# Exponentials bank by bank and sums in two halves in a windowed-attention softmax

## The chip, the core and the metric

The kernel runs on one core of one Trainium2 chip. The metric is the device time of one execution in microseconds (us); the time before is the median of three runs. One further execution was recorded by the hardware profiler, and all profile lines come from it. Engines are named as the profile names them: PE is TensorE's matrix multiplication and PEld its weight load, DVE is VectorE, ACT is ScalarE, POOL is GpSimd and SP is SyncE.

## The reference

The program is a chain of four residual blocks on an input of 4 x 1024 x 128: a selective state-space scan ("mamba"), a layer of eight experts with two chosen for each token, a dynamic convolution over 31 positions, and a transformer of six layers. Only the transformer's attention is touched:

```python
def local_attention(q, k, v):
    ...
    sim = jnp.einsum('bhwie,bhwje->bhwij', bq, bk2) * QK_SCALE
    sim = jnp.where(mask, -jnp.finfo(sim.dtype).max, sim)
    attn = jax.nn.softmax(sim, -1)
    out = jnp.einsum('bhwij,bhwje->bhwie', attn, bv2)
    return out.reshape(b, h, n, d)
```

There are 16 heads of 64 channels and windows of 32 positions; each position looks at its own window and the one before it, 64 keys in all. So for a tile of 128 positions the softmax is over 128 x 16 rows of 64 values. The kernel computes it as usual: the maximum of a row, the differences to it, their exponentials, the sum of these, and the product with the sum's reciprocal.

## The kernel before

**Tiling.** The transformer works on 192 tiles: 4 sequences by 6 layers by 8 tiles of 128 positions. The loop in `run` (line 1501) takes one tile i per turn. In a turn it turns queries and keys of tile i by transposes (`turn`), makes the scores and the softmax of tile i (`scores`, line 1328), mixes the values of tile i - 1 with its softmax (`mix`, line 1387), and projects tile i + 2 to queries and keys (`project`, line 1256). After every fourth tile a feed-forward block of 512 positions follows, spread over the turns (`feedforward`). Beside the tiles, `along` lets three lines of other work advance a share at a time: mamba, experts and convolution of the later sequences, and the preparation of later layers' weights. That work is used up before the end, so the last tiles run with nothing beside them.

**The softmax of a tile.** `scores` holds the scores in two PSUM banks (`sv`, tile name `sim` in the code, `bank` in the profile): bank e has the even or the odd heads, 8 heads x 64 keys = 512 values in each of 128 partitions. For each bank VectorE takes the maximum into `mx` and subtracts it into `at` (lines 1355 to 1362). `at` is one SBUF buffer of 128 x 1024 values, ordered head pair, bank, key; the half of one bank is 8 pieces of 64 values with a stride of 128. Two such buffers are used in turn. Then follow, over all 1024 values: one exponential on ScalarE (line 1364), one sum over each row of 64 on VectorE into `sm` (line 1366), the reciprocal of the 16 sums (line 1367), and one product on POOL (line 1368). `mix` transposes `at` on PE, ScalarE copies it to `aT`, PE multiplies it with the values into two banks at a time, ScalarE copies these to `zT`, and PE multiplies `zT` with the joined value and output weights `wvo`.

**What else is on these engines.** `project` makes, for each of four half-sized matrix products of a tile: one square on ScalarE (`sq`), two products with the rotary tables on VectorE (`r`, `rb`), one sum of the squares on VectorE (into `words`). Then POOL adds `r` and `rb`, VectorE finds 32 inverse roots in small steps (`root`, `ne`, `words`), and POOL multiplies `r` with them. `feedforward` has three Gelu functions for each 512 positions (`ge`), and the experts have them too (`ehg`). ScalarE holds one table of functions at a time; a change between the table with Exp and that with Gelu is an instruction of its own (ACT_TABLE_LOAD in the profile). The copies and squares are not tied to a table in the planner's accounts.

**Who sets the order.** No call in these functions goes to an engine directly. The class `Order` takes each operation as a unit with its engine, its cost (`length`, line 248), the units that it depends on (by exact sets of elements, so that two strided halves of one buffer do not touch) and its PSUM banks. `arrange` (line 278) then plans the whole program at once: at each step it gives out the unit that can start earliest, among those that start nearly as early the one first written, with limits on free banks and on how far ahead it may look (500 units). A unit that needs another function table than the one loaded counts 1.28 us later (line 319). `give` (line 369) issues the units in the planned order, each engine's queue in order; the waits between engines are drawn from the dependencies. As every instruction is issued on line 374, the profile's groups all bear that line and are told apart by tile names. The planner counts a reduction on VectorE of n values, up to 1024, at 0.07 + 0.00104 n us, and a function on ScalarE at 0.25 + 0.00045 n us up to 512 values and 0.25 + 0.0007 n above.

Of the kernel before, what the change touches and what calls it, by code (L numbers as in the profile page):

```python
# [10 lines left out]
F32 = mybir.dt.float32  # L11
BF16 = mybir.dt.bfloat16
I32 = mybir.dt.int32
AF = mybir.ActivationFunctionType
ALU = mybir.AluOpType
AX = mybir.AxisListType
PSUM = bass.MemoryType.PSUM

P = 128
# [11 lines left out]
DEPTH, HEADS, DH, WIN = 6, 16, 64, 32  # L31
# [1118 lines left out]
class Transformer:  # L1150
# [177 lines left out]
    def scores(self, t, qT, kT):  # L1328

        nc, c = self.nc, self.c
        m = self.mask[:, 0 if t == 0 else 1, None, :].to_broadcast([P, 8, 2 * WIN])
        sv = [c.bank("sim").rearrange("p (a k) -> p a k", k=2 * WIN) for e in range(2)]
        with nc.together(2.0):
            for e in range(2):
                nc.tensor.matmul(
                    sv[e], self.identb, m, start=True, stop=False, skip_group_check=True
                )
            for a in range(8):  # L1340
                for g in range(4):
                    for e in range(2):
                        rows = slice(e * 64, (e + 1) * 64)
                        cols = slice(g * WIN, (g + 1) * WIN)
                        nc.tensor.matmul(
                            sv[e][cols, a, :],
                            qT[rows, a, cols],
                            kT[rows, a, g * WIN : (g + 2) * WIN],
                            start=False,
                            stop=True,  # L1350
                            skip_group_check=True,
                        )
        mx = self.sb.tile([P, 2, 8], F32, "mx", bufs=3)
        at = self.sb.tile([P, 8, 2, 2 * WIN], F32, "at", bufs=2)
        for e in range(2):
            nc.vector.tensor_reduce(out=mx[:, e, :], in_=sv[e], op=ALU.max, axis=AX.X)
            nc.vector.tensor_tensor(
                out=at[:, :, e, :],
                in0=sv[e],
                in1=mx[:, e, :, None].to_broadcast([P, 8, 2 * WIN]),  # L1360
                op=ALU.subtract,
            )
        av = at.rearrange("p a e k -> p (a e) k")
        nc.scalar.activation(av, av, AF.Exp)
        sm = self.sb.tile([P, HEADS], F32, "sm", bufs=3)
        nc.vector.tensor_reduce(out=sm, in_=av, op=ALU.add, axis=AX.X)
        nc.vector.reciprocal(sm, sm)
        nc.gpsimd.tensor_tensor(
            out=av, in0=av, in1=sm[:, :, None].to_broadcast([P, HEADS, 2 * WIN]), op=ALU.mult
        )  # L1370
        return at
# [359 lines left out]
```

## Time and profile before

| what | value |
|---|---|
| time, median of three runs | 4260.55 us (4259.56 to 4266.35) |
| the profiled execution's time | 4259.06 us |
| its span in the trace | 4257.2 us |
| instructions in it | 112033 |
| mean granted clock of PE | 0.948 |

How to read what follows. A line with percentages gives each engine's busy time in us, its share of the span and the number of its instructions. The rows of forty digits cut the span into equal slices of 106 us, each digit being the busy share in tenths. A row of a group gives the engine, the operation, output and input by name, their shapes and the count; then, behind the bar, the total busy time in us and the mean of one instruction in ns; then, behind the next bar, the time that the engine stood idle just before such instructions and what ended most of it. A row of the waits gives who waited, for whom, the total in us, the number of times and the longest. Duration and pace differ: on VectorE and ScalarE the next instruction can begin before the last one's recorded end.

### The profile page before, as it was taken

The page shows a single profiled execution, that of the slowest core. Times are in us where ns is not written, and L with a number is a line of the kernel's source. Part 1 is how long each engine was busy: PE and PEld are TensorE (multiplying, and loading weights), DVE is VectorE, ACT ScalarE, POOL GpSimd, SP SyncE. Part 2 cuts the span into 40 slices and gives each one's busy share as a digit, 9 for nine tenths or more (in the row PEclk, how much of TensorE's full clock was granted, in tenths as well). Part 3 has the DMA queues.
Part 4 walks back from the last instruction along what each step waited for, and adds up shares of the span by engine and source line. Part 5 has one row for each costly group of instructions (what it writes and reads, how often), then busy time and mean ns, then how long its engine had stood idle before and what let it go on. Part 6 is the DMA issues. An engine that isn't in the chain of part 4 may idle for free. (4 is left out here: it accounts for less than half of the span.)

```text
span 4257.2 us, 112033 instructions
## 1 busy us (share of the span) xinstructions
PE 3801.6 (89%) x45306; PEld 2721.5 (64%) x45317; DVE 3612.4 (85%) x9374; ACT 2610.7 (61%) x4854; POOL 2964.5 (70%) x1832
## 2 busy tenths in 40 slices
PE   3874788998988999988999999999999999999997
PEld 1762465675665666656676677766666777777775
DVE  4668789888997879999998787898989898888985
ACT  3754466675555777655667676666665666666664
POOL 3388667666878766777789665788688666666663
PEclk6886899999998999989999999999999999999998
DMA  3323321222112221111113122121111010101100
GB/s 91 104 83 123 119 85 43 86 62 72 60 68 82 91 73 55 45 57 53 44 63 114 58 65 63 41 73 59 58 61 51 27 41 25 32 21 34 33 27 11
DMA packets 136878, 261.25 MB, mean 61 GB/s; under 512 B 16112, under 2 KB 93992, under 8 KB 129192
## 3 DMA queue, kind: packets, MB, share of 16 engines
q1 hardware_dynamic: 123352, 211.47, 15.0%
q0 software_dynamic: 13008, 42.62, 3.2%
q8 instruction: 357, 5.85, 0.6%
q14 instruction: 161, 1.32, 0.1%
HBM read 224.41 MB, written 29.62 MB: 60 GB/s over the span
## 5 line engine op out<-in xcount | busy, mean ns | idle before, releaser
L374 POOL TENSOR_TENSOR r<-r,rb 128x1024 f32<-128x1024 f32 x384 | 906.9, 2367 | 365.2 <-DVE rb L374 297.9
L374 POOL TENSOR_TENSOR r<-r,root 128x1024 f32<-128x1024 f32 x384 | 723.2, 1903 | 181.2 <-DVE root L374 154.4
L374 PE MATMUL bank<-wqk,hs 128*128 128x512 f32 x1536 | 769.7, 624 | 45.0 <-DVE at L374 13.3
L374 PEld LDWEIGHTS bank<-zT,wvo 128*128 128x128 f32 x6144 | 723.2, 194 | 88.8 <-issue 53.2
L374 PE MATMUL bank<-zT,wvo 128*128 128x128 f32 x6144 | 729.4, 277 | 6.5 <-ACT zT L374 3.5
L374 ACT ACTIVATE sq<-bank 128x512 f32<-128x512 f32 x768 | 450.4, 601 | 458.1 <-DVE words L374 228.1
L374 ACT COPY zT<-bank 128x512 f32<-128x512 f32 x768 | 403.7, 597 | 382.4 <-PE bank L374 376.6
L374 DVE TENSOR_TENSOR r<-bank,rot 128x512 f32<-128x512 f32 x768 | 522.0, 680 | 103.4 <-issue 36.2
L374 POOL TENSOR_TENSOR at<-at,sm 128x1024 f32<-128x1024 f32 x192 | 365.4, 1903 | 326.2 <-DVE sm L374 146.3
L374 DVE TENSOR_TENSOR rb<-bank,rot 128x512 f32<-128x512 f32 x768 | 520.8, 678 | 62.8 <-ACT sq L374 53.8
L374 DVE TENSOR_REDUCE words<-sq 128x8 f32<-128x512 f32 x768 | 526.5, 686 | 14.3 <-ACT sq L374 5.3
L374 PEld LDWEIGHTS bank<-wqk,hs 128*128 128x128 f32 x1536 | 267.6, 195 | 322.7 <-issue 157.7
L374 PE MATMUL bank<-aT,xw 64*128 64x256 f32 x3072 | 430.6, 404 | 25.4 <-DVE at L374 10.3
L374 PE MATMUL bank<-ident,r 128*128 128x128 f32 x3080 | 400.6, 278 | 45.1 <-DVE rb L374 10.0
L374 PEld LDWEIGHTS bank<-ident,r 128*128 128x128 f32 x3080 | 350.1, 143 | 134.9 <-issue 59.7
L374 PEld LDWEIGHTS bank<-aT,xw 64*128 64x128 f32 x3072 | 295.6, 192 | 153.2 <-issue 44.3
L374 PEld LDWEIGHTS bank<-kT,qT 64*32 64x32 f32 x24576 | 259.7, 106 | 106.8 <-issue 105.4
L374 PE MATMUL bank<-kT,qT 64*32 64x64 f32 x24576 | 296.6, 227 | 12.4 <-issue 11.9
L374 DVE TENSOR_REDUCE mx<-bank 128x8 f32<-128x512 f32 x384 | 254.1, 680 | 44.4 <-PE bank L374 44.3
L374 PE MATMUL bank<-fxn,w 128*128 128x512 f32 (+1 forms) x576 | 272.8, 607 | 7.0 <-ACT fxn L374 4.8
L374 ACT ACTIVATE at<-at 128x1024 f32<-128x1024 f32 x192 | 203.5, 1060 | 117.6 <-DVE at L374 83.2
L374 ACT COPY qT<-bank 128x512 f32<-128x512 f32 x384 | 228.3, 600 | 66.2 <-PE bank L374 62.8
(207 smaller groups left out, 6849.8 us busy)
## 6 DMA issues: line engine op xcount, KB each, us to landing
near<-rows SPq DMA_DIRECT2D x31, 1024.0 KB
near<-rows SPq DMA_DIRECT2D x31, 960.0 KB
rot<-rotd SPq DMA_DIRECT2D x192, 128.0 KB
wqk<-in_Wqkv SPq DMA_DIRECT2D x48, 512.0 KB
wvo<-wvod SPq DMA_DIRECT2D x24, 1024.0 KB
ewt<-in_w_ex SPq DMA_DIRECT2D x16, 514.0 KB
w<-in_W SPq DMA_DIRECT2D x24, 341.0 KB
wvod<-eT SPq DMA_DIRECT2D x24, 256.0 KB
```

The costliest lines, as they stand in the source:

```text
L374: getattr(engine, op)(*map(real, args), **{k: real(v) for k, v in kw.items()})
```

## The change

The exponential over both banks becomes one for each bank, written directly behind that bank's subtraction. The sum over all 16 heads becomes two sums over 8 heads, one for each bank, written after both; each writes every second value of `sm`. The reciprocal and the product stay as they are. The values computed are the same.

```diff
         mx = self.sb.tile([P, 2, 8], F32, "mx", bufs=3)
         at = self.sb.tile([P, 8, 2, 2 * WIN], F32, "at", bufs=2)
+        sm = self.sb.tile([P, HEADS], F32, "sm", bufs=3)
+        sums = sm.rearrange("p (a e) -> p a e", e=2)
         for e in range(2):
             nc.vector.tensor_reduce(out=mx[:, e, :], in_=sv[e], op=ALU.max, axis=AX.X)
             nc.vector.tensor_tensor(
@@ -1360,10 +1362,10 @@
                 in1=mx[:, e, :, None].to_broadcast([P, 8, 2 * WIN]),
                 op=ALU.subtract,
             )
+            nc.scalar.activation(at[:, :, e, :], at[:, :, e, :], AF.Exp)
+        for e in range(2):
+            nc.vector.tensor_reduce(out=sums[:, :, e], in_=at[:, :, e, :], op=ALU.add, axis=AX.X)
         av = at.rearrange("p a e k -> p (a e) k")
-        nc.scalar.activation(av, av, AF.Exp)
-        sm = self.sb.tile([P, HEADS], F32, "sm", bufs=3)
-        nc.vector.tensor_reduce(out=sm, in_=av, op=ALU.add, axis=AX.X)
         nc.vector.reciprocal(sm, sm)
         nc.gpsimd.tensor_tensor(
             out=av, in0=av, in1=sm[:, :, None].to_broadcast([P, HEADS, 2 * WIN]), op=ALU.mult
```

## The prediction

> **What bounds the kernel now.** I read the busy table of the page first, then its slices, then the table of stretches, and only then the groups. Busy time and slices say that no engine is the bound throughout:
>
> ```profile
> PE 3801.6 (89%) x45306; PEld 2721.5 (64%) x45317; DVE 3612.4 (85%) x9374; ACT 2610.7 (61%) x4854; POOL 2964.5 (70%) x1832
> ...
> PE   3874788998988999988999999999999999999997
> PEld 1762465675665666656676677766666777777775
> DVE  4668789888997879999998787898989898888985
> ```
>
> The table of stretches (start:end, then busy us of PE, PEld, DVE, ACT, POOL, then clock, DMA share and GB/s) separates the two parts in which the softmax runs:
>
> ```profile
> 600.00:3400.00 2800.00, 2586.64 (x31617) 1852.36 (x31627) 2456.19 (x6357) 1790.24 (x3366) 2072.56 (x1262) 0.97 0.19 62
> 3400.00:4200.00 800.00, 786.17 (x10510) 577.92 (x10495) 711.82 (x1811) 507.59 (x900) 512.36 (x289) 1.00 0.09 29
> ```
>
> In the last 800 us PE is busy for 98.3% (786.17 of 800): nothing to be had but 13.8 us. In the 2800 us before it, where mamba, experts and conv run beside the tiles, PE is idle for 213.4 us and VectorE for 343.8 us. What PE waited for, over the whole span (engine waiting, releaser, us, times, longest):
>
> ```profile
> PE bank L374 <- DVE m L374: 63.7, 52, 11.4
> PE bank L374 <- DVE at L374: 38.7, 40, 5.2
> ...
> PE bank L374 <- ACT zT L374: 13.1, 25, 1.2
> ...
> PE bank L374 <- POOL at L374: 8.6, 12, 2.5
> ```
>
> The second row is a wait for the subtraction, which frees the score bank; the change does not touch when a subtraction may begin. The last two are what it can shorten: POOL's product is the end of the softmax, and the exp stands ahead of copies to zT in ScalarE's queue. Together 21.7 us.
>
> **The change, part by part.** The rows are these, counts and mean ns ahead of and behind the bar's busy time:
>
> ```profile
> L374 ACT ACTIVATE at<-at 128x1024 f32<-128x1024 f32 x192 | 203.5, 1060 | 117.6 <-DVE at L374 83.2 <-DVE ne L374 19.8 <-DVE words L374 5.6
> L374 DVE TENSOR_REDUCE sm<-at 128x16 f32<-128x1024 f32 x192 | 232.5, 1211 | 28.8 <-ACT at L374 27.1
> ...
> L374 ACT ACTIVATE ew<-ew 128x496 f32<-128x496 f32 x32 | 19.8, 620 | 42.3 <-DVE ew L374 36.0 <-DVE ne L374 6.1
> ```
>
> *The sums.* 192 reductions of 128x1024 go, 384 of 128x512 come. The nearest row is the reduction of sq in `project`, also from SBUF, 768 times at 686 ns. By durations: 2 x 686 - 1211 = +161 ns, 30.9 us in all. But durations overlap on VectorE, as the timeline shows:
>
> ```profile
> 3878.49 1.21 DVE L374 TENSOR_REDUCE sm<-at 128x16 f32<-128x1024 f32 x1
> 3879.61 0.68 DVE L374 TENSOR_REDUCE words<-sq 128x8 f32<-128x512 f32 x1
> 3880.20 0.24 DVE L374 RECIPROCAL sm<-sm 128x16 f32<-128x16 f32 x1
> ```
>
> The instruction after a full sum starts 1.12 us later, that after a half-sized one 0.59 us later; the medians of all such pairs that I read are 1.13 and 0.60. So a tile costs 2 x 0.60 - 1.13 = +0.07 us of VectorE, 13.4 us over 192 tiles. Here a rule speaks against the change: the Trainium skill, Perfetto Trace Analysis, section "Optimizing Scalar/DVE Operations", gives each VectorE instruction about 60 ns of data access on SBUF and each ScalarE one about 93 ns, and advises grouping work into larger operations where an engine is saturated. By it the sums cost 192 x 60 ns = 11.5 us, by the row 13.4; I take the row. The rule's condition is what matters: VectorE is at 88% (2456.19 of 2800) in the mixed part and 89% in the last. In the mixed part some 135 of the 192 tiles run (the products by window), so all of it on the path would be 135 x 0.07 = 9.5 us; in the last part PE covers it. I take half, **+5 us** (ends 0, if all is hidden, and +22, which is 135 x 161 ns).
>
> *The exps.* 192 of 128x1024 go, 384 of 128x512 come. By the row of ew (128x496) 2 x 620 - 1060 = +180 ns, in pace 2 x 0.53 - 0.96 = +0.10 us, so 19 us of ScalarE (the same rule would say 17.9). ScalarE is busy 64% in the mixed part and 63% in the last, so PE's and VectorE's work hide this; were that cover gone it would be 19 us, 35 by the durations.
>
> *The gain.* A softmax is shorter from the second subtraction to the product: about 0.43 us of exp (0.96 - 0.53), as the first half runs beside the second maximum and subtraction, and, where VectorE is free, the first sum beside the second exp (another 0.5 us). The chain of waits shows where the exp alone holds PE:
>
> ```profile
> 3689.86 1.21 DVE at L374 x2
> ...
> 3691.14 1.06 ACT at L374
> 3692.20 0.48 ACT zT L374
> ```
>
> The copy to zT waits behind the exp, the exp for both subtractions; with halves zT starts some 0.4 us sooner, if the planner leaves it there. In 62 of 192 tiles the instruction after the exp on ScalarE is such a copy. A third of the 13.1 us behind zT is 4.2 us; of the 8.6 us behind the product I count 2, since before many products the sum stands in VectorE's queue behind r, rb and words long after its exp is done. **-6 us** (ends 0 and -21.7).
>
> *The waits.* ScalarE's second exp waits for the second subtraction while sq (93 tiles) or zT (62) is queued behind it, as behind the one exp now; the new one is the first exp's wait for its own subtraction. What follows the first exp may now be held for up to the 1.3 us of maximum and subtraction, if the plan puts both exps side by side. VectorE's first sum waits for the first exp, its second for the second; behind them stand r, rb and words, on which the squares' buffers and POOL's r wait. The 28.8 us of idle time before the sum is what that costs now, and halves can lengthen or shorten it; I take zero net. The reciprocal follows the second sum at once, as it followed the full one. POOL and DMA issue nothing new; the loop over banks moves no transfer past SP or POOL.
>
> *Table loads.* There are 195, 1283 ns each. A Gelu planned between the two exps costs up to two more. In 20 tiles a Gelu stands between the first subtraction's end and the exp. The planner charges 1.28 us to whatever changes the table, so it will rarely split a pair: 0 to 20 x 2 x 1.283 = 51 us of ScalarE; five splits, 13 us, mostly in its idle third: **+2 us**. The skill's ScalarE: Activation LUTs, section "Table sets: the hidden batching unit", says to keep calls of one set together and puts a switch at about 2.7 us; the trace's row is 1.28, so the five splits would be 27 us by the page and 13 by the row.
>
> *The order.* All instructions of all engines come from one plan, and 384 units more of other lengths in it move everything behind them. No row shows that. Bounds: in the last 800 us a better order can win at most 13.8 us; a worse one, with PE as idle as in 3200 to 3400 us (188.69 of 200, 5.7%), loses 32 us; in the mixed part a tenth more or less of PE's 213 us is 21 us either way. The asymmetry of the PE-bound part decides: a third of the 32, **+10 us**.
>
> Sum: 5 - 6 + 2 + 10 = +11 us on the profiled execution's 4259.06 us (span 4257.2), so **4270 us**; the median of the runs, 4260.55, lies 1.5 us above that execution, and I leave this inside the rounding. About 0.2% (8.5 us) is what a measurement of this kernel can tell from no change.
>
> **The rivals.** *Hidden* (23%): the longer sums lie in VectorE's idle time, the order comes out as good, 4260 us. For it: 85% and 61% busy; against: any new order is a throw of more than 8 us. *Shorter chain* (22%): the 21.7 us behind zT and the product go almost whole and the mixed part gains a few us more, about -25, 4235 us. For it: POOL idles 146 us for the sum; against: POOL is not the bound, and the sum is late by VectorE's queue. *Broken rhythm* (13%), on the other side of that: ScalarE stands on its first exp's or second exp's wait with zT behind it, so PE waits for its bank. Price 0.25 us in each of 192 tiles, 48 us, 4308 us; it decides from some 0.1 us a tile, where it alone passes the term for the order. The same price follows if the strided halves of one buffer were ordered against each other, the second subtraction waiting for the first exp: 0.62 + 0.1 of signal - 0.60 of maximum = 0.12 us a tile, 23 us on VectorE. In that case the change does not do what it says. Forecast (small loss): 42%.
>
> So slower by over 0.2% is 0.42 + 0.13 = 0.55, within 0.23, faster 0.22. Range: from near the shorter chain to the broken rhythm, 4238 to 4312; the forecast's own is 4269 to 4290.
>
> **What would show it.** Right: sums at 384 x some 0.68 us, VectorE's busy time up by about 31 us and ScalarE's by about 35, PE at less than 98% in the last 800 us, up to ten more table loads. Wrong: PE's waits for zT and for the product gone with the span below 4250; or table loads up by 20 or more; or second subtractions that VectorE begins only after the first exp ended.

## The result, and the profile after

The changed kernel takes 4281.74 us (median of 5 runs, 4279.02 to 4286.13) against 4259.56 us (4252.49 to 4266.35): ratio 1.0054, 95% interval 1.0041 to 1.0067. It is slower, and about 23 us is to be explained (17 to 29 by the interval). Its profiled execution took 4279.02 us, with a span of 4277.2, 20.0 us above that of before. The busy table:

```profile
PE 3825.2 (89%) x45317; PEld 2726.2 (64%) x45317; DVE 3635.5 (85%) x9566; ACT 2624.8 (61%) x5046; POOL 2970.2 (69%) x1832
```

VectorE is busy 23.1 us longer and ScalarE 14.1 us; both shares of the span are what they were. The table of stretches:

```profile
600.00:3400.00 2800.00, 2588.72 (x31462) 1848.59 (x31461) 2457.82 (x6462) 1792.62 (x3486) 2070.36 (x1258) 0.97 0.19 63
3400.00:4200.00 800.00, 788.56 (x10444) 574.26 (x10429) 719.82 (x1846) 503.71 (x937) 507.95 (x286) 1.00 0.09 29
```

Read the counts, not the busy times. In the last 800 us PE looks busier than before (788.56 for 786.17 us), but it did 10444 matrix products for 10510, and POOL 286 operations for 289: a little less work in the same time. The comparison is rough, as the changed kernel is some 18 us behind by then and the 800 us hold a slightly different piece of it. The softmax's groups and the waits of PE that the prediction named:

```profile
L374 DVE TENSOR_REDUCE sm<-at 128x8 f32<-128x512 f32 x384 | 251.1, 677 | 9.8 <-ACT at L374 8.0
L374 ACT ACT_TABLE_LOAD x195 | 250.2, 1283 | 100.0 <-DVE at L374 96.0 <-PEq L1721 0.7 <-DVE m L374 0.3
L374 ACT ACTIVATE at<-at 128x512 f32<-128x512 f32 x384 | 232.0, 630 | 182.5 <-DVE at L374 123.8 <-DVE ne L374 32.9 <-DVE words L374 23.5
```

```profile
PE bank L374 <- DVE at L374: 43.9, 32, 9.2
...
PE bank L374 <- DVE rb L374: 41.6, 42, 4.9
...
PE bank L374 <- ACT zT L374: 17.4, 32, 1.4
...
PE bank L374 <- POOL at L374: 3.9, 3, 2.7
```

The halves have the lengths that were forecast. Table loads are 195, as before, but ScalarE now stands 100.0 us in front of them, where it stood 4.1. The subtractions end 96.0 us of this, 26 waits of at most 4.1 us: in these tiles the load ahead of a first half-exp starts only once a subtraction is done. Here the first half-exp was planned early, ahead of copies to zT, after a Gelu:

```profile
3871.97 0.69 ACT L374 ACTIVATE ge<-bank,b 85x512 f32<-85x512 f32 x1 [0.17 <-PE bank L374]
3876.62 1.28 ACT L374 ACT_TABLE_LOAD   x1 [3.96 <-DVE at L374]
3877.91 1.15 ACT L374 ACTIVATE at<-at 128x512 f32<-128x512 f32 x2
3878.97 2.03 ACT L374 COPY zT<-bank 128x512 f32<-128x512 f32 x4
```

In another tile both half-exps came between the second and the third copy to zT. The chain of waits there runs through the exps and that copy into PE, which stood 0.19 us for it (start, us, what; in the kernel before, the chain is PE's own work there, 33.12 us from 3827.23):

```profile
3857.32 1.24 ACT at L374 x2
3858.57 0.48 ACT zT L374
3859.05 0.04 issue
3859.09 4.87 PE bank L374 x35
```

That made a tempting story: the first exp, brought forward, blocks ScalarE's queue. What PE stood for it directly is small, though: its waits for zT rose by 4.3 us in all, from 13.1 to 17.4. The experiments had to say whether the story was the loss.

### The profile page after: what moved, and what is told of

The parts are those of the page before. It is cut to its first block, busy times and chain, and to the rows that moved or that the text cites. A ratio compares the mean times of both kernels' runs of the same rounds, so it can differ in the third digit from the quotient of the medians.

```text
span 4277.2 us, 112319 instructions
## 1 busy us (share of the span) xinstructions
PE 3825.2 (89%) x45317; PEld 2726.2 (64%) x45317; DVE 3635.5 (85%) x9566; ACT 2624.8 (61%) x5046; POOL 2970.2 (69%) x1832
## 4 chain that ended last, share of the span: by engine, by line
DVE 37%; PE 30%; ACT 7%; issue 4%; POOL 1%; DMA 1%; ACTq 0%; POOLq 0%; DVEq 0%; SPq 0%
PE bank L374 30%; DVE words L374 8%; DVE rb L374 6%; DVE r L374 6%; DVE sm L374 3%; DVE mx L374 2%; DVE ne L374 2%; DVE hs L374 2%; ACT sq L374 2%; DVE at L374 2%; DVE cxn L374 1%; DVE m L374 1%; DVE st L374 1%; ACT at L374 1%; ACT zT L374 1%
## 5 line engine op out<-in xcount | busy, mean ns | idle before, releaser
L374 PE MATMUL bank<-wqk,hs 128*128 128x512 f32 x1536 | 785.0, 632 | 63.3 <-DVE at L374 26.0
L374 ACT ACTIVATE at<-at 128x512 f32<-128x512 f32 x384 | 232.0, 630 | 182.5 <-DVE at L374 123.8
L374 PE MATMUL bank<-kT,qT 64*32 64x64 f32 x24576 | 297.3, 228 | 11.6 <-issue 11.5
```

The costliest lines, as they stand in the source:

```text
L374: getattr(engine, op)(*map(real, args), **{k: real(v) for k, v in kw.items()})
```

## The experiments

Times drift a little between comparisons, so each run is read as its ratio to the kernel before, run beside it on the same chip.

### The plan and the instructions taken apart

A unit of the planner holds a list of calls. Exchanging the calls after the unit has been recorded keeps the plan and changes what is issued. In the first trace below every instruction of ScalarE, VectorE, POOL and PE's weight loads stands where it stood before, each pair counted as one.

**old_plan_halves**, from the kernel before:

```diff
-        nc.scalar.activation(av, av, AF.Exp)
+        u = nc.scalar.activation(av, av, AF.Exp)
+        u.calls = [("activation", (at[:, :, e, :], at[:, :, e, :], AF.Exp), {}) for e in range(2)]
...
-        nc.vector.tensor_reduce(out=sm, in_=av, op=ALU.add, axis=AX.X)
+        u = nc.vector.tensor_reduce(out=sm, in_=av, op=ALU.add, axis=AX.X)
+        u.calls = [
+            ("tensor_reduce", (), dict(out=sums[:, :, e], in_=at[:, :, e, :], op=ALU.add, axis=AX.X))
+            for e in range(2)
+        ]
```

> Half-sized exps and half-sized sums stand in the place of the whole ones, in the plan of the kernel before: every other instruction of every engine keeps its place. Theory ORDER (the 0.54% come from the new plan): ratio to before 0.998 to 1.002, 4252 to 4268 us, since the added 13 us of VectorE and 19 us of ScalarE are mostly hidden. Theory COST (more instructions and waits are the loss, wherever they stand): ratio 1.004 to 1.007, 4277 to 4289 us.

Measured: 0.9990 (0.9984 to 0.9997), 4244.44 us beside 4248.0. The halves alone do not cost; they gain a tenth of a per cent, about 4 us. Its groups:

```profile
L374 ACT ACT_TABLE_LOAD x195 | 250.2, 1283 | 4.1 <-PEq L1725 0.7
L374 DVE TENSOR_REDUCE sm<-at 128x8 f32<-128x512 f32 x384 | 243.9, 677 | 14.8 <-ACT at L374 14.3
L374 ACT ACTIVATE at<-at 128x512 f32<-128x512 f32 x384 | 227.9, 630 | 68.8 <-DVE at L374 59.2 <-DVE words L374 3.9 <-DVE ne L374 2.9
```

With the pairs side by side, 192 pairs of sums take 243.9 us, 11.4 us more than the 232.5 us of the whole sums, and the exps 24.4 us more than 203.5. In exchange the first exp need not wait for the second subtraction. One tile in its timeline, VectorE's rows and ScalarE's:

```profile
3864.03 0.69 DVE L374 TENSOR_TENSOR at<-bank,mx 128x512 f32<-128x512 f32 x1
3865.35 0.69 DVE L374 TENSOR_TENSOR at<-bank,mx 128x512 f32<-128x512 f32 x1
3867.76 1.27 DVE L374 TENSOR_REDUCE sm<-at 128x8 f32<-128x512 f32 x2
```

```profile
3865.35 1.36 ACT L374 ACTIVATE at<-at 128x512 f32<-128x512 f32 x2
```

The exps begin at 3865.35 with the second subtraction, where a whole exp would have begun behind its end, at 3866.04 or later. Idle time in front of the exps falls from 117.6 to 68.8 us, in front of the sums from 28.8 to 14.8.

**new_plan_wholes**, from the changed kernel:

```diff
-            nc.scalar.activation(at[:, :, e, :], at[:, :, e, :], AF.Exp)
+            u = nc.scalar.activation(at[:, :, e, :], at[:, :, e, :], AF.Exp)
+            u.calls = [("activation", (av, av, AF.Exp), {})] if e else []
...
-            nc.vector.tensor_reduce(out=sums[:, :, e], in_=at[:, :, e, :], op=ALU.add, axis=AX.X)
+            u = nc.vector.tensor_reduce(out=sums[:, :, e], in_=at[:, :, e, :], op=ALU.add, axis=AX.X)
+            u.calls = [("tensor_reduce", (), dict(out=sm, in_=av, op=ALU.add, axis=AX.X))] if e else []
```

> The plan of the changed kernel, but issued with whole instructions: one exp of 128x1024 where the second half-exp stands, one sum of 128x1024 where the second half-sum stands, nothing where the first halves stood. Theory ORDER: 1.003 to 1.007, 4272 to 4289 us, as the changed kernel. Theory COST: 0.998 to 1.002, 4252 to 4268 us.

Measured: 1.0257 (1.0244 to 1.0270), 4354.48 us. Both theories missed the size. COST falls twice over: fewer and larger instructions in the new plan are 2% slower than the changed kernel itself (1.0257 / 1.0054). ORDER forecast the sign alone. The new plan counts on the second exp and the second sum being short, and puts PE's and ScalarE's next work right behind them; issued whole, they must end later. PE's waits and the idle time in front of the sum (9.8 us in the changed kernel) agree with that:

```profile
L374 DVE TENSOR_REDUCE sm<-at 128x16 f32<-128x1024 f32 x192 | 234.0, 1219 | 104.9 <-ACT at L374 102.3
...
PE bank L374 <- DVE rb L374: 54.8, 73, 4.8
...
PE bank L374 <- ACT zT L374: 38.5, 60, 2.3
```

So the four corners are:

| | whole instructions | halves |
|---|---|---|
| plan of before | 1 | 0.9990 |
| plan of the change | 1.0257 | 1.0054 |

In either plan the halves are the faster ones, so they are not what costs. In the plan of before they cost nothing, and the loss comes with the new plan. The corner 1.0257 does not measure that plan alone: it holds instructions that the plan was not made for.

### One half of the change at a time

**exp_halves_only** keeps the exp in the loop over banks and restores the whole sum; **sum_halves_only** keeps the two sums and restores one exp. Both are planned anew.

```diff
# exp_halves_only, from the changed kernel
-        for e in range(2):
-            nc.vector.tensor_reduce(out=sums[:, :, e], in_=at[:, :, e, :], op=ALU.add, axis=AX.X)
+        nc.vector.tensor_reduce(out=sm, in_=av, op=ALU.add, axis=AX.X)
# sum_halves_only, from the changed kernel (the line that makes av moves up)
-            nc.scalar.activation(at[:, :, e, :], at[:, :, e, :], AF.Exp)
+        nc.scalar.activation(av, av, AF.Exp)
```

> Only the exps by bank, each after its own subtraction; the sum stays whole; planned anew. Theory ORDER: any new plan is a throw, so anything from 0.997 to 1.008, and not tied to the 13 us of VectorE that this one does not add. Theory COST: ScalarE's 19 us are hidden, so 0.999 to 1.002, the loss being in the sums.

> Only the sums in two halves after one whole exp; planned anew. Theory ORDER: anything from 0.997 to 1.008. Theory COST: VectorE's added 13 to 31 us are the loss, so 1.003 to 1.007, 4272 to 4289 us.

Measured: 1.0040 (1.0027 to 1.0053) and 1.0069 (1.0056 to 1.0082). Each part alone costs about what both together do; they do not add. COST wanted the exps free and missed; its figure for the sums fits, but old_plan_halves has shown that the same sums in place cost nothing. ScalarE's stand in front of the table loads appears with the split exps alone and not with the split sums, and yet the split sums are no faster. The row of exp_halves_only, then that of sum_halves_only:

```profile
L374 ACT ACT_TABLE_LOAD x196 | 251.5, 1283 | 78.6 <-DVE at L374 67.7 <-DVE ne L374 6.5 <-PEq L1719 0.7
L374 ACT ACT_TABLE_LOAD x189 | 242.5, 1283 | 4.0 <-PEq L1721 0.7
```

That is the first evidence against the story of the first exp: a loss of this size needs no such wait.

### Other plans for unchanged instructions

These three issue the instructions of the kernel before, not one added, and only tell the planner another length of the whole sum:

```diff
-        nc.vector.tensor_reduce(out=sm, in_=av, op=ALU.add, axis=AX.X)
+        nc.vector.tensor_reduce(out=sm, in_=av, op=ALU.add, axis=AX.X).cost += 0.01
```

with +0.01, -0.01 and +0.07 us.

> The instructions of the kernel before, none added or split; the planner is merely told that the whole sum takes 10 ns more than it did (1.145 for 1.135 us), so it writes out another order. Theory LOTTERY (a new plan as such costs about 0.5%, whatever prompts it, because the order before was a good draw): 1.002 to 1.010, 4257 to 4290 us. Theory SOFTMAX (the loss is particular to first exps brought forward or to halved sums in the order): 0.998 to 1.002.

> As null_sum_plus_010ns, with the planner told 10 ns less (1.125 us). Theory LOTTERY: 1.002 to 1.010, and not the same as for 10 ns more. Theory SOFTMAX: 0.998 to 1.002.

> The instructions of the kernel before; the planner is told that the whole sum takes 70 ns more (1.205 us, what it counts for two halves). Theory LOTTERY: 1.002 to 1.010, like the other two. Theory SOFTMAX: 0.998 to 1.002. A third reading, that the planner's longer VectorE time alone makes its order worse: clearly slower than the two with 10 ns.

Measured: 0.9986 (0.9978 to 0.9994), 0.9962 (0.9948 to 0.9976) and 1.0057 (1.0040 to 1.0074). SOFTMAX falls, as a new plan moves the time by more than its interval with no instruction split. LOTTERY as it was put falls as well: a new plan does not cost half a per cent as such, since two of three were faster than the one before. What stands is that the order alone is worth from -0.4% to +0.6% here, which is the size of the whole effect. 70 ns more counted for the sum, what the two halves count more, gives 1.0057 with none of the change's instructions.

### The first exp

**exps_after_both** writes both half-exps behind the loop, after both subtractions.

```diff
-            nc.scalar.activation(at[:, :, e, :], at[:, :, e, :], AF.Exp)
+        for e in range(2):
+            nc.scalar.activation(at[:, :, e, :], at[:, :, e, :], AF.Exp)
```

> Both halves of exp and sum as in the changed kernel, but the two exps are written after both subtractions, not each after its own; planned anew. Theory SOFTMAX (the first exp brought forward, with table load and copies to zT held behind it on ScalarE, is the loss): 0.998 to 1.002, and ScalarE's wait of 100 us at table loads gone. Theory LOTTERY: 1.002 to 1.010 with or without that wait.

Measured: 1.0043 (1.0027 to 1.0060), and ScalarE still stands 99.8 us in front of the table loads. The edit did not do what it was to do: the order in which units are written settles only near ties, and the first exp depends on the first subtraction alone, so it was planned as early as before. In the two traces ScalarE, VectorE, POOL and PE's weight loads have the same instructions in the same order, so this run is in effect the changed kernel measured a second time: 1.0043 for 1.0054, with overlapping intervals. To hold the exp back an edge is needed. **exps_held** has it:

```diff
+        for e in range(2):
+            half = nc.scalar.activation(at[:, :, e, :], at[:, :, e, :], AF.Exp)
+            nc.edge(last, half)
```

where `last` is the second subtraction's unit.

> The changed kernel with one more edge in the planner: neither half-exp may be planned before the second subtraction, so the pair stands side by side on ScalarE. Planned anew. Theory FIRST EXP (the first exp planned early, with its table load and the copies to zT held behind it, is a lasting loss in the tiles without other work): from product 144 to product 191 no longer than the kernel before, within 3 us, where the changed kernel loses 3 to 8; ScalarE's wait at table loads 5 us for 100. Theory DRAW (the loss is how the order falls): the sum of the mixed part's shifts is open, total 0.996 to 1.007.

Measured: 1.0093 (1.0079 to 1.0107), the wrong way. The wait did go:

```profile
L374 ACT ACT_TABLE_LOAD x191 | 245.1, 1283 | 4.7 <-PEq L1723 0.7 <-DVE at L374 0.7
...
PE bank L374 <- ACT zT L374: 11.6, 21, 1.4
```

ScalarE's 100 us in front of table loads are gone, PE's waits for zT are shorter than before the change, and the kernel is slower still. So a plan without the wait can lose more than the one with it, and the split sums and the plan with 70 ns more lost about as much without it. ScalarE has over a third of its time to spare. What the wait cost in the changed kernel is not shown by this: exps_held is planned anew, and the draw of its order can hide a few us won. From product 144 to product 191 exps_held loses 2.8 us and the changed kernel 3.3, both within the margin of FIRST EXP, so that part of the expectation told nothing apart. DRAW gave 0.996 to 1.007 and 1.0093 lies outside: the spread of plans is wider than I had put it.

### Is it the time that the planner counts?

> The changed kernel's instructions; the planner counts each half-sum 0.5675 us, so that both together cost it what the whole sum did (1.135). Theory PLANNED TIME (the planner's 70 ns more of VectorE per tile make its order worse): 0.997 to 1.002. Theory DRAW: anything from 0.996 to 1.007, no nearer to 1 than the changed kernel's 1.0054 on principle.

> The instructions of the kernel before, the planner told that the whole sum takes 140 ns more. Theory PLANNED TIME: worse than with 70 ns more (1.0057), so 1.007 to 1.014. Theory DRAW: anything from 0.996 to 1.007.

The first is the changed kernel with `.cost = 0.5675` behind each half-sum, the second the kernel before with `+= 0.14`. Measured: 1.0073 (1.0059 to 1.0086) and 1.0111 (1.0096 to 1.0126). With unchanged instructions the ratios for 10, 70 and 140 ns more are 0.9986, 1.0057 and 1.0111: they rise with the counted time, as PLANNED TIME says, although the first of them lies below the 1 of the plan with nothing added. But taking the 70 ns out of the changed kernel's plan made it no better (1.0073 for 1.0054), which speaks against it. The cause that makes one plan worse than another is not settled.

### Where on the way the time goes

POOL's product at<-at,sm occurs once per tile, in the same sequence in every kernel. Read from the timelines, its start in before, and how much later it starts in the others (us; one profiled execution each, so some 10 us of a row can be the run's own level):

```
product   before  change  old_plan  null   null   null   exps_
                          _halves   -10    +70    +140   held
  0        314.0   +2.1    -1.7    -0.4   +0.2   -1.0   -1.4
 24       1004.4  +21.8    -0.1    +4.3   -1.1  +31.8  +28.4
 48       1557.6   +6.5    -4.3   -10.5   -9.6  +20.7  +15.2
 72       2078.0  +13.4    -5.7    -6.8   +5.9  +30.5  +29.3
 96       2547.4   +9.8    -9.8   -12.1   +5.5  +36.5  +36.9
120       2990.2  +15.9    -9.9   -12.0   +4.2  +41.1  +35.3
144       3422.1  +18.3    -9.6    -4.4  +23.7  +39.1  +36.3
168       3829.7  +14.1   -10.6   -11.6  +25.4  +43.0  +34.2
191       4210.6  +21.6   -12.1    -8.3  +25.5  +40.8  +39.1
```

Plans win and lose in steps, at different places: the change loses 20 us up to product 24, wins 15 back by 48, and loses again; null +70 is ahead by 9.6 us at product 48 and loses 20 between 120 and 144. From product 144 to 191, with next to no work beside the tiles, no column moves by more than 4 us: these losses come where mamba, experts and convolution are woven in. It is no rule for every plan, as of the kernels not shown exp_halves_only loses 7 us there and new_plan_wholes 41 of its 97. Old_plan_halves has no such steps; most of its 12 us are the level of its chip, where the kernel before took 4248.0 us.

The granted clock of PE is a rival that the experiments did not hold fixed. Among runs of the kernel before, a mean clock lower by 0.001 goes with 1.7 to 2.4 us more (three series of 11 to 27 runs). The changed kernel's five runs have 0.9456 on average, the profile of before 0.948, so by an estimate from these figures the clock goes with some 5 of its 22 us. It is not the whole: exp_halves_only is slower at a higher clock (a mean of 0.953 for 0.950), and between products 0 and 24, where the change loses 20 us, the clock is 0.89 in both. Half of what null -10 gains goes with its higher clock (0.952 for 0.948). Whether a plan moves the clock or the clock moves beside it, no run shows.

### A faster version

**halves_in_better_plan** is old_plan_halves with the sum counted 10 ns less.

> Half-sized exps and sums put in the place of the whole ones in the plan of null_sum_minus_010ns. If both effects add (0.9962 by the plan, 0.9990 by the halves in place): 0.995, 4236 to 4244 us at the level of the last comparison, faster than the kernel before and the changed one. If they do not: 0.996 to 1.000.

Measured: 0.9974 (0.9962 to 0.9985), 4245.4 us beside 4255.86. It beats the kernel before and the changed one, but the two gains did not add: the plan alone gave 0.9962, and the intervals overlap, so in that plan the halves are worth nothing that can be told.

## Why the prediction came out as it did

The side, slower, was right and the time is in the range, and also in the forecast's own 4269 to 4290; the size was twice the forecast, +23 us for +11. Of the signs named for it only the length of the sums came in full: VectorE's busy time rose by 23.1 us and not 31, ScalarE's by 14.1 and not 35, and PE's share in the last 800 us did not fall. None of the three signs of being wrong came.

- *Sums, +5; exps, covered.* The durations were right (677 ns for some 680, 630 for 620), and so was the pace: 11.4 us over 192 pairs for 13.4. But the added work was not on the path: old_plan_halves is faster although its groups hold 11.4 us more of VectorE and 24.4 us more of ScalarE work. The Trainium skill's rule of larger operations (Perfetto Trace Analysis, "Optimizing Scalar/DVE Operations"), weighed there, came near the engines' cost, 11.5 us for the sums' 11.4 and 17.9 for the exps' 24.4 in old_plan_halves; it does not give the kernel's time.
- *Gain, -6.* About right where the plan is kept: together with the costs above, -4 us (-7 to -1) was measured for the +1 that the three own terms (5, -6, 2) summed to. In the changed kernel no gain shows: PE's waits for zT and for the product sum to 21.3 us, for 21.7 before.
- *Table loads, +2.* None was added, the count is 195 in both. Instead the load took on the first exp's wait, 96.0 us on ScalarE. I had named a first exp that blocks its queue as the rival that would cost 48 us; it did block, and PE's waits for zT rose by 4.3 us. Plans without the block lost as much or more; its own share of the loss was not measured apart.
- *Order, +10.* This is the term that was mis-sized. With the halves' own -4 taken off, the new plan cost about 27 us. Its bounds (21 us either way in the mixed part, 13.8 won to 32 lost in the last) were fair for the change but too narrow for other plans, which reached +1.1% (about 47 us). Its reason was wrong: I put the loss into the last 800 us, where PE has no slack, and the last 48 products moved by 3.3 us; PE's share there did not fall below 98% but rose to 98.6. Some 18 of the 21.6 us had arisen by product 144. As the other three terms made +1 us in the forecast and measured -4, the side hung on this term alone; it came out right for a reason that did not hold, which is luck.
- *The strided halves.* The rival in which they are ordered against each other did not occur: the 384 subtractions of old_plan_halves have 0.5 us of idle time ahead of them in all, as before, and in the timeline above the first exp and the second subtraction run at the same time. The prediction put this rival at "the same price" as the broken rhythm, 48 us; its own sum makes 23.

What stays open is why this plan is a worse one: no single wait was found that carries the 27 us, the clock goes with a part of them, and the two experiments on the planner's counted time contradict each other.

## What to carry to other kernels

Where a program plans the order of all engines at once, every edit is two edits: its instructions and a new order. Measure them apart, by issuing the new instructions in the old plan, and set a few null changes of the planner's costs beside them: if these alone move the time by as much as the edit, the edit has told you nothing about itself. And a wait that a trace shows in plain sight, even 100 us of it, is not yet the loss: see what PE waited because of it (4.3 us for zT here), and take it away in an order that otherwise stays, which these experiments did not do.

## What the runs showed of the hardware

In these traces the wait of an exp is carried by the table load in front of it: the load is not done ahead of time while the data is still coming. In the changed kernel 96.0 of the 100.0 us of idle time before loads end with the subtraction; where no first exp was brought forward it is 4.0 to 5.1 us in all. The switch itself cost what its row says: 1.28 us, with the first exp starting 0.01 us behind the load (3876.62 + 1.28 to 3877.91). And PE's busy time rose by 23.6 us over the span for the same matrix products (45306 and 45317 of them recorded), so that it cannot be read as work done. The lower clock, 0.946 for 0.948, would make some 8 us of that by proportion, an estimate; the rest has no cause on record.
